# One sequence of scan rounds for all images, with a fixed share of other work between the sums of two rounds

## The chip, the core and the metric

The kernel runs on one core of a Trainium2 chip. The time is that of one launch on the device in microseconds, from several executions. All data are float32.

## What is computed

Eight images of 384 channels and 32 x 32 pixels go through four layers. Layer 0 is a Mamba block in both directions beside a local gate; its core, for each channel and each of 16 states, is a recurrence over the 1024 pixels:

```python
def step(h, inp):
    dA, dBu, c = inp
    h = dA * h + dBu
    return (h, jnp.einsum('bdn,bn->bd', h, c))
...
y = ys.transpose(1, 0, 2) + u * D_param
y = y * silu(z)
...
local_feat = jax.nn.sigmoid(conv + dw_b[None, :, None, None]) * x_norm
return x + res_scale * (global_feat + local_feat)
```

Layer 1 is a 1x1 convolution, a 3x3 depthwise one, another 1x1, a linear attention with eight heads and an MLP of 384 to 1536 to 384 with GELU. Layer 2 is a sum of depthwise convolutions (merged into one of 13 x 13), layer 3 a 1x1 and again a 13 x 13 depthwise convolution with GELU. Layers 2 and 3 come at the end for all images together.

## The kernel before

The program is written in a layer that records instructions with their data dependences, and then orders them on each engine by a list scheduler with its own model of times. Each engine (TensorE is PE, VectorE DVE, ScalarE ACT, GpSimd POOL, SyncE SP) then runs its list in order, and waits on semaphores where an input or a buffer isn't ready. Records made earlier have the higher priority, but what is ready first in the model goes first.

Four generators make the work of layers 0 and 1. A generator yields a number after each piece, its cost in units of about one dense product.

- `front(b)`, 90 units: the norm of image b, the input projection (`in`), the local gate (tiles `lc`, `lg`; conv3, L511; activation L615, products L618 and L619), the 1-D convolution (`ut`, `c1`, `uc`), the projections `xd` and `dt`, softplus (Abs, ReLU, Exp, Ln; L671 to L678) and the products for the scan (L683 to L689). It writes `dl_d`, `v_d`, `bc_d`, `ud_d`, `z_d` to device memory.
- `scan(b)`: the recurrence, in 12 units (two directions, two halves of 512 pixels, three groups of 128 channels) of four rounds each: 48 rounds an image. A round handles 4 of the 16 states for 128 channels, which gives 512 rows: two tiles (i = 0, 1) of two halves.
- `layer1(b)`, 325 units: out-projection (`op`), first 1x1 (`h`), depthwise (`dw`), second 1x1 (`c2`), keys and values (`kv`), queries (`q`), normalizer (`den`, `rz`, `rzb`), projection (`pj`), mean and variance (`mu`, `var`), and the MLP: 24 steps of a product `mf`, GELU (`hm`, L1062) and three products `mo` (L1064).
- `fold()` and `kernels` fold normalizations into weights and merge the convolutions' kernels, once.

A round of the scan, for each of the two tiles: ACT makes two exponentials `da` (L776), DVE a product `du` (L781, into PSUM) and two scans `hs` (L793), POOL multiplies by C in place (L802). Two rounds later PE adds over the states: four matmuls with a constant selector, each on 32 columns of the array (`sums`, L736), into one accumulator `acc`; in a unit's first round also an identity product (L741). After a unit's last round ACT (L746) or DVE (L749) takes `acc` away. There are four buffers of `da` (two rounds), eight of `hs` (four rounds), one of `du`, one of `acc`. Matmul results of the other work go to two PSUM buffers `mm` and three `mo`. The inputs of a depthwise or 1-D convolution are copied by DMA into `im` tiles, six of them, four for one convolution.

The driving loop runs the scan of image b and records, after each round, pieces of the front of image b+1 and of layer 1 of image b-1, in proportion to the rounds done. At the image's end it records all that is left, and the next image's scan starts anew, with its own loads. PE's order of sums against other products is left to the scheduler. The front of image 0 runs ahead of all, layer 1 of image 7 alone after all, then the convolutions (L316).

Of the kernel before, what the change touches and what calls it, by code (L numbers as in the profile page):

```python
# [36 lines left out]
N_A6, N_T2, N_S2, N_W, N_IM = 7, 11, 3, 4, 6  # L37
N_REP, N_DA, N_HS = 6, 4, 8
TP = H * (KP // 2)
PADW = KS // 2  # L40
# [334 lines left out]
def _layers01(tc, nc, B, xv, x2_d, dram, ident, mean_w, eps5, eps6, one, half, minus1, vec, bns, bnt,  # L375
# [12 lines left out]
    with ExitStack() as ctx:  # L388
# [30 lines left out]
        def const(ap, shape, tag):  # L419
            t = wp.tile(shape, FP, tag=tag, name=tag)  # L420
            nc.scalar.dma_start(t, ap)
            return t
# [10 lines left out]
        t1 = const(taps1, [P, 2 * NG, 32], "t1")  # L433
        selt = const(sel, [P, 32], "selt")
        neg_a = const(alog, [P, NG, NR], "neg_a")
        nc.scalar.activation(neg_a, neg_a, AF.Exp)
# [56 lines left out]
        def tick(everything=False):  # L493
            for e in list(late):
                e[0] -= 1
                if e[0] < 0 or everything:
                    late.remove(e)
                    e[1]()

        def dense(ps, w, m, rhs):  # L500
# [71 lines left out]
        def front(b):  # L572
# [36 lines left out]
            for h in range(2):  # L609
                for c in range(NC):  # L610
                    xr = t2(f"xr_{b}_{h}_{c}")
                    nc.sync.dma_start(xr, xv[b][:, c, bass.ts(h, HALF)])
                    ps = conv3(xn_d, b % 2, h, c, t3, f"lc_{b}_{h}_{c}")
                    lc = t2(f"lg_{b}_{c}_{h}")
                    nc.scalar.activation(lc, ps, AF.Sigmoid, bias=vec("dw_b0", c))  # L615

                    def local(h=h, c=c, lc=lc, xr=xr):
                        nc.vector.tensor_mul(rows(lc), rows(lc), xn[h][c])  # L618
                        nc.vector.scalar_tensor_tensor(xr, lc, rs, xr, ALU.mult, ALU.add)  # L619
                        nc.gpsimd.dma_start(x1v[b][:, c, bass.ts(h, HALF)], xr)  # L620

                    defer(1, local)
                    yield 3
# [70 lines left out]

        def scan(b):

            units = [
                (d, h, c)
                for d in range(2) for h in ((0, 1) if d == 0 else (1, 0)) for c in range(NC)
# [6 lines left out]
            def load_bc(k, r):  # L706
                d, h, _ = units[k]
                t = sp.tile([P, 2, HALF], FP, tag="bct", name=f"bct_{b}_{d}_{h}_{r}", bufs=4)
                for o in range(2):
                    src = bass.AP(  # L710
                        bc_d.tensor, bc_d[b, d, o * NST + 4 * r, h * HALF].offset,
                        [[0, 32], [L, 4], [1, HALF]],
                    )
                    nc.sync.dma_start(t[:, o, :], src)
                return t

            def load(k, i):

                d, h, c = units[k]
                ts = []  # L720
                for src_d, n in ((dl_d, "dlt"), (v_d, "vr")):
                    t = sp.tile([P, 2 * HALF], FP, tag="rep", name=f"{n}_{b}_{d}_{h}_{c}_{i}", bufs=N_REP)
                    for j in range(2):
                        src = bass.AP(
                            src_d.tensor, src_d[b, d, P * c + 32 * (2 * i + j), h * HALF].offset,
                            [[L, 32], [0, 4], [1, HALF]],
                        )
                        nc.sync.dma_start(t[:, bass.ts(j, HALF)], src)
                    ts.append(t)
                return ts  # L730

            def sums(k, r, hs, acc, y0, zt):
                d, h, c = units[k]
                cols = bass.ts(h, HALF)
                for j in range(4):
                    nc.tensor.matmul(  # L736
                        acc[32 * j : 32 * j + 32, :], selt, hs[j // 2][:, bass.ts(j % 2, HALF)],
                        start=(r == 0), stop=(r == NR - 1), skip_group_check=True,
                    )
                if r == 0:  # L740
                    nc.tensor.matmul(acc, ident, y0, start=False, stop=False, skip_group_check=True)  # L741
                if r < NR - 1:
# [11 lines left out]
            acc = y0 = zt = nxt = None  # L754
            for k, (d, h, c) in enumerate(units):
                cols = bass.ts(h, HALF)
                second = k % (2 * NC) >= NC
                for r in range(NR):
# [12 lines left out]
                    for i in range(2):  # L771
                        dlt, vt = now[i]
                        da = sp.tile([P, 2 * HALF], FP, tag="da", name=f"da_{b}_{k}_{r}_{i}", bufs=N_DA)
                        for j in range(2):
# [4 lines left out]
                            )  # L779
                        du = accp.tile([P, 2 * HALF], FP, tag="du", name=f"du_{b}_{k}_{r}_{i}")  # L780
                        nc.vector.tensor_mul(  # L781
# [5 lines left out]
                        if i == 0 and k and c == 0 and r == 0:  # L787
                            bct[NR - 1] = load_bc(k, NR - 1)
                        t = sp.tile([P, 2 * HALF], FP, tag="hs", name=f"hs_{b}_{k}_{r}_{i}", bufs=N_HS)
                        for j in range(2):  # L790
# [86 lines left out]
        def layer1(b):  # L877

            xx = []
            w = wtile(outproj_t, f"wo_{b}")  # L880
            for h in range(2):
                xh, gh = a6(f"xx_{b}_{h}"), a6(f"g_{b}_{h}")
                nc.sync.dma_start(xh, x1v[b][:, :, bass.ts(h, HALF)])
                nc.sync.dma_start(gh, gv[b][:, :, bass.ts(h, HALF)])
                xx.append(xh)
                for m in range(NC):
# [5 lines left out]
            w = wtile(c1_d, f"c1_{b}")  # L892
            for h in range(2):
                hh, mid = image6(f"hh_{b}_{h}")
# [195 lines left out]
        tick(everything=True)  # L1090
        rounds = 4 * NC * NR
        for b in range(B):
            work = []
            if b + 1 < B:
                work.append([front(b + 1), 90, 0])
            if b > 0:
                work.append([layer1(b - 1), 325, 0])
            if b == 0:
                work.append([fold(), 30, 0])
            if b == 1:  # L1100
                work.append([some(prepare, 7), 1, 0])
            elif b > 1:
                work.append([some(prepare, 6), 12, 0])
            need = sum(n for _, n, _ in work)
            done = 0
            for i, _ in enumerate(scan(b)):
                tick()

                while work and done < need * (i + 1) / (rounds - 1):
                    w = min(work, key=lambda w: w[2] / w[1])  # L1110
                    cost = next(w[0], None)
                    if cost is None:
                        work.remove(w)
                        continue
                    w[2] += cost
                    done += cost
            for w in work:
                for _ in w[0]:
                    tick()
            tick(everything=True)  # L1120
        for _ in prepare:
# [92 lines left out]
```

## Time and profile before

| | us |
|---|---|
| median of 3 runs (5799.74 to 5806.63) | 5803.92 |
| profiled execution: time | 5806.88 |
| profiled execution: span | 5805.1 |
| PE, DVE, ACT, POOL busy | 4813.5, 3677.1, 3064.5, 2892.9 |
| granted clock of TensorE, mean | 0.896 |

Times of a group are of single instructions; a float32 matmul appears as two entries (two passes). The ends of matmuls are modelled and overlap, so a group's busy time is shorter than count times mean. "Idle before" is what the engine waited ahead of the group, with what ended it.

### The profile page before, as it was taken

The page shows a single profiled execution, that of the slowest core. Times are in us where ns is not written, and L with a number is a line of the kernel's source. Part 1 is how long each engine was busy: PE and PEld are TensorE (multiplying, and loading weights), DVE is VectorE, ACT ScalarE, POOL GpSimd, SP SyncE. Part 2 cuts the span into 40 slices and gives each one's busy share as a digit, 9 for nine tenths or more (in the row PEclk, how much of TensorE's full clock was granted, in tenths as well). Part 3 has the DMA queues.
Part 4 walks back from the last instruction along what each step waited for, and adds up shares of the span by engine and source line. Part 5 has one row for each costly group of instructions (what it writes and reads, how often), then busy time and mean ns, then how long its engine had stood idle before and what let it go on. Part 6 is the DMA issues. An engine that isn't in the chain of part 4 may idle for free. (4 is left out here: it accounts for less than half of the span.)

```text
span 5805.1 us, 57844 instructions
## 1 busy us (share of the span) xinstructions
PE 4813.5 (83%) x19550; PEld 2091.8 (36%) x19550; DVE 3677.1 (63%) x3775; ACT 3064.5 (53%) x4116; POOL 2892.9 (50%) x1603
## 2 busy tenths in 40 slices
PE   4576579977988799879888997899779869899999
PEld 1121124322332243223322332233223324498498
DVE  0399997968687768776878786878678811011211
ACT  1656546874667557846784687468635613000211
POOL 3277676557554656565656564656466700110133
PEclk7687689988999899989999998899889989999999
DMA  9555476677567756764666467646643541366677
GB/s 299 185 176 178 145 247 194 230 188 216 187 197 202 216 173 193 168 204 134 191 205 189 141 175 186 190 140 176 179 145 120 135 96 45 95 165 158 196 166 150
DMA packets 528255, 1012.16 MB, mean 174 GB/s; under 512 B 60616, under 2 KB 196248, under 8 KB 527960
## 3 DMA queue, kind: packets, MB, share of 16 engines
q1 hardware_dynamic: 387952, 665.99, 38.5%
q0 software_dynamic: 71136, 248.53, 16.6%
q10 hardware_dynamic: 68872, 93.95, 5.1%
q8 instruction: 155, 2.54, 0.2%
q14 instruction: 140, 1.15, 0.1%
HBM read 763.86 MB, written 288.36 MB: 181 GB/s over the span
## 5 line engine op out<-in xcount | busy, mean ns | idle before, releaser
L802 POOL TENSOR_TENSOR hs<-hs,bct 128x1024 f32<-128x1024 f32 x768 | 2378.7, 3098 | 1180.4 <-DVE hs L793 665.8
L776 ACT ACTIVATE da<-dlt,neg_a 128x512 f32<-128x512 f32 x1536 | 1031.7, 714 | 848.8 <-DVE hs L793 756.8
L793 DVE TENSOR_TENSOR_SCAN hs<-da,carry,du 128x512 f32<-128x512 f32 x768 | 947.1, 1268 | 445.8 <-PE acc L736 211.0
L781 DVE TENSOR_TENSOR du<-vr,bct 128x1024 f32<-128x1024 f32 x768 | 1048.3, 1365 | 51.7 <-issue 21.7
L793 DVE TENSOR_TENSOR_SCAN hs<-da,du 128x512 f32<-128x512 f32 x768 | 901.2, 1208 | 153.9 <-ACT da L776 74.0
L736 PE MATMUL acc<-hs,selt 128*32 128x512 f32 x3072 | 736.5, 674 | 293.0 <-POOL hs L802 241.7
L1064 PE MATMUL mo<-hm,w 128*128 128x512 f32 x1152 | 562.5, 628 | 84.4 <-ACT hm L1062 60.8
L502 PE MATMUL mf<-ln,w 128*128 128x512 f32 x1152 | 545.7, 614 | 42.8 <-ACT dl L672 40.4
L736 PEld LDWEIGHTS acc<-hs,selt 128*32 128x32 f32 x3072 | 122.3, 115 | 722.2 <-POOL hs L802 391.6
L1064 PEld LDWEIGHTS mo<-hm,w 128*128 128x128 f32 x1152 | 214.9, 197 | 427.8 <-issue 255.1
L776 ACT ACT_TABLE_LOAD x265 | 340.0, 1283 | 39.2 <-DVE hs L793 26.7
L502 PEld LDWEIGHTS mf<-ln,w 128*128 128x128 f32 x1152 | 215.2, 194 | 358.9 <-issue 285.1
L316 PE MATMUL cv_b<-xt_b,toep 128*64 128x256 f32 x2688 | 304.5, 388 | 14.1 <-DVE xt_b L298 14.1
L316 PE MATMUL cv_a<-xt_a,toep 128*64 128x256 f32 x2688 | 304.6, 388 | 9.2 <-DVE xt_a L298 9.2
L502 PE MATMUL in<-xn,win 128*128 128x512 f32 x576 | 289.1, 633 | 26.0 <-ACT phi_k L874 24.2
L511 PE MATMUL dw<-dw_i,t3b 96*32 96x512 f32 x1152 | 238.0, 707 | 86.4 <-DMA dw_i<-h_d 86.3
L316 PEld LDWEIGHTS cv_b<-xt_b,toep 128*64 128x64 f32 x2688 | 282.5, 199 | 36.6 <-issue 16.2
L316 PEld LDWEIGHTS cv_a<-xt_a,toep 128*64 128x64 f32 x2688 | 282.4, 199 | 31.1 <-issue 10.4
L511 PE MATMUL lc<-lc_i,t 96*32 96x512 f32 x1152 | 218.1, 679 | 57.2 <-issue 28.8
L511 PE MATMUL c<-ut,t 128*32 128x512 f32 x768 | 195.2, 676 | 45.6 <-DMA ut<-u_d 32.1
L502 PE MATMUL op<-g,wo 128*128 128x512 f32 x288 | 143.1, 647 | 86.7 <-DMA g<-g_d 58.7
L1062 ACT ACTIVATE hm<-mf,biasf 128x512 f32<-128x512 f32 x192 | 130.7, 687 | 145.2 <-PE mf L502 143.5
(189 smaller groups left out, 5618.3 us busy)
## 6 DMA issues: line engine op xcount, KB each, us to landing
dlt<-dl_d SPq DMA_DIRECT2D x384, 256.0 KB, 4.5
vr<-v_d SPq DMA_DIRECT2D x384, 256.0 KB, 4.7
bct<-bc_d SPq DMA_DIRECT2D x256, 256.0 KB, 4.1
ut<-u_d SPq DMA_DIRECT2D x192, 257.5 KB, 5.0
lc_i<-xn_d SPq DMA_DIRECT2D x192, 228.8 KB, 4.9
dw_i<-h_d SPq DMA_DIRECT2D x192, 228.8 KB, 4.1
tp_d<-g_d POOLq DMA_DIRECT2D x64, 672.0 KB, 7.2
w<-w_d SPq DMA_DIRECT2D x64, 576.0 KB, 5.8
```

The costliest lines, as they stand in the source:

```text
L316: nc.tensor.matmul(ps[2 * H * e : 2 * H * (e + 1), 0:BW], tp[:, 2 * (g % (GB // 2)) + e, :, :, t].rearrange("p c j -> p (c j)"), rhs, star ...
L502: nc.tensor.matmul(ps, w[:, k, m * P : (m + 1) * P], rhs[k] if isinstance(rhs, list) else rhs[:, k, :], start=(k == 0), stop=(k == NC - 1),)
L511: nc.tensor.matmul(ps[32 * j : 32 * j + 32, :], lhs(j, i), rhs(j, i), start=(i == 0), stop=(i == taps - 1), skip_group_check=True,)
L736: nc.tensor.matmul(acc[32 * j : 32 * j + 32, :], selt, hs[j // 2][:, bass.ts(j % 2, HALF)], start=(r == 0), stop=(r == NR - 1), skip_group ...
L776: nc.scalar.activation(da[:, bass.ts(j, HALF)], dlt[:, bass.ts(j, HALF)], AF.Exp, scale=neg_a[:, g, r : r + 1],)
L781: nc.vector.tensor_mul(pairs(du), pairs(vt), bct[r][:, 0:1, :].to_broadcast([P, 2, HALF]),)
L793: nc.vector.tensor_tensor_scan(t[:, s][:, way], da[:, s][:, way], du[:, s][:, way], k_c if second else 0.0, ALU.mult, ALU.add,)
L802: nc.gpsimd.tensor_mul(pairs(t), pairs(t), bct[r][:, 1:2, :].to_broadcast([P, 2, HALF]))
L1062: nc.scalar.activation(hm, ps, AF.Gelu, bias=biasf[:, NC * i + f, :])
L1064: nc.tensor.matmul(acc[m], wb[:, f, m * P : (m + 1) * P], hm, start=(i == 0 and f == 0), stop=(i == FF // C - 1 and f == NC - 1),)
```

## The change

The program has one generator `scan()` that runs through the rounds of all eight images, with the buffers, the loads ahead and the two rounds of lag carried over the boundary. The driving loop takes one round at a time and then records each generator's share on its own, by the round's place between `lo` and `hi`: the front from round 0 to 43, layer 1 from 3 to 47. What it records is placed on PE behind the last sums recorded (`issue_after`), and the next sums behind the last PE instruction of each generator in that round (`order`); both are edges of order only, without a wait on a result. So on PE the sums of one round, one round's pieces, and the sums of the next round follow each other. `LAG` and `BEHIND` are constants that would loosen this.

Two further edits: the local gate's sigmoid is made from tanh, sigmoid(v) = (tanh(v/2) + 1)/2, with halved bias and residual scale (four small DVE products at the start); and layer 1 handles half 1 ahead of half 0 in its first two products, since the second direction's scan finishes half 1 first.

```diff
-                    nc.scalar.activation(lc, ps, AF.Sigmoid, bias=vec("dw_b0", c))
+                    nc.scalar.activation(lc, ps, AF.Tanh, bias=dwh[:, c, :], scale=0.5)
...
-                        nc.vector.tensor_mul(rows(lc), rows(lc), xn[h][c])
-                        nc.vector.scalar_tensor_tensor(xr, lc, rs, xr, ALU.mult, ALU.add)
+                        nc.vector.scalar_tensor_tensor(
+                            rows(lc), rows(lc), one, xn[h][c], ALU.add, ALU.mult
+                        )
+                        nc.vector.scalar_tensor_tensor(xr, lc, rsh, xr, ALU.mult, ALU.add)
...
-        def scan(b):
+        def scan():
             units = [
-                (d, h, c)
+                (b, d, h, c) for b in range(B)
                 for d in range(2) for h in ((0, 1) if d == 0 else (1, 0)) for c in range(NC)
             ]
...
+                after = between[-BEHIND] if len(between) >= BEHIND else []
                 for j in range(4):
-                    nc.tensor.matmul(
+                    ins = nc.tensor.matmul(
                         acc[32 * j : 32 * j + 32, :], selt, hs[j // 2][:, bass.ts(j % 2, HALF)],
                         start=(r == 0), stop=(r == NR - 1), skip_group_check=True,
                     )
+                    for o in after:
+                        order(ins.ins, o)
...
+                summed.append(ins.ins)
...
-            for h in range(2):
+            for h in (1, 0):
...
+        last = rounds - NR + 1
...
+                work.append([front(b + 1), 90, 0, last - 2, 0])
...
+                work.append([layer1(b - 1), 325, 3, rounds - 1, 0])
...
-            for i, _ in enumerate(scan(b)):
+            for i in range(rounds):
+                next(scans)
                 tick()
-                while work and done < need * (i + 1) / (rounds - 1):
-                    w = min(work, key=lambda w: w[2] / w[1])
...
-            for w in work:
-                for _ in w[0]:
-                    tick()
-            tick(everything=True)
+                ends = []
+                with tc.issue_after(summed[-1 - LAG]) if len(summed) > LAG else nullcontext():
+                    for w in list(work):
+                        gen, need, lo, hi, done = w
+                        at = len(traced())
+                        while done < need * (i + 1 - lo) / (hi - lo) or i >= hi:
+                            cost = next(gen, None)
...
+                        mine = [t for t in traced()[at:] if t.engine == mybir.EngineType.PE]
+                        if mine:
+                            ends.append(mine[-1])
+                between.append(ends)
```

## The prediction

> **What bounds the kernel now.** I read the stages first: the windows of the trace cut where a new image's scan starts (the first POOL product of each image gives the times), then the groups of the page, then the timeline of single rounds, then the waits of the tiles `hs`, `hm` and `dw_i`.
>
> ```profile
> core 0: us, PE busy (x) PEld busy (x) DVE busy (x) ACT busy (x) POOL busy (x), PEclk, DMA share, GB/s
> 0.00:227.10 227.10, 120.44 (x390) 34.41 (x392) 29.77 (x80) 67.10 (x90) 56.63 (x111) 0.73 0.87 275
> 227.10:738.20 511.10, 312.44 (x1000) 82.98 (x996) 442.17 (x424) 312.15 (x423) 330.10 (x157) 0.69 0.49 163
> ...
> 2461.10:3029.70 568.60, 481.74 (x1720) 174.49 (x1720) 440.89 (x435) 379.55 (x497) 330.92 (x157) 0.94 0.59 179
> ...
> 4170.10:4650.60 480.50, 393.71 (x1292) 146.18 (x1292) 392.73 (x386) 255.03 (x350) 311.25 (x121) 0.91 0.48 136
> 4650.60:5040.00 389.40, 314.11 (x912) 135.72 (x910) 32.17 (x52) 72.37 (x107) 22.88 (x30) 0.89 0.30 74
> 5040.00:5805.10 765.10, 734.39 (x5664) 620.14 (x5664) 129.07 (x192) 100.75 (x192) 153.67 (x182) 0.98 0.67 165
> ```
>
> Rows: front of image 0; scan of image 0; scan of image 4 (images 1 to 6 are like it: 581, 546, 596, 569, 566, 575 us); scan of image 7; layer 1 of image 7 alone; the convolutions. In the middle images PE is busy 85%, DVE 78%, ACT 67%: three engines close together, so 48 rounds of 11.8 us each are neither PE's nor DVE's sum alone. The spacing of the POOL products shows rounds from 7.6 us (nothing but DVE) to 42 us (image 4, 17th round: over 90 other matmuls stand between two sums). So work is lumped.
>
> ```profile
> L776 ACT ACTIVATE da<-dlt,neg_a 128x512 f32<-128x512 f32 x1536 | 1031.7, 714 | 848.8 <-DVE hs L793 756.8
> ...
> L793 DVE TENSOR_TENSOR_SCAN hs<-da,carry,du 128x512 f32<-128x512 f32 x768 | 947.1, 1268 | 445.8 <-PE acc L736 211.0
> ...
> L736 PE MATMUL acc<-hs,selt 128*32 128x512 f32 x3072 | 736.5, 674 | 293.0 <-POOL hs L802 241.7
> ...
> L776 ACT ACT_TABLE_LOAD x265 | 340.0, 1283 | 39.2 <-DVE hs L793 26.7
> ...
> L1062 ACT ACTIVATE hm<-mf,biasf 128x512 f32<-128x512 f32 x192 | 130.7, 687 | 145.2 <-PE mf L502 143.5
> ```
>
> Here a ring is seen: ACT's exponentials wait for DVE's scans (four `da` buffers, two rounds), DVE's scans wait for PE's sums (eight `hs` buffers, four rounds). One round in the timeline gives its prices:
>
> ```profile
> 2705.22 1.06 PE L736 MATMUL acc<-hs,selt 128*32 128x512 f32 x8
> ...
> 2706.22 7.99 PE L502 MATMUL q<-xx,wq 128*128 128x512 f32 x18
> ...
> 2706.49 2.45 DVE L793 TENSOR_TENSOR_SCAN hs<-da,carry,du 128x512 f32<-128x512 f32 x2 [3.62 <-PE acc L736]
> ...
> 2708.97 1.23 DVE L781 TENSOR_TENSOR du<-vr,bct 128x1024 f32<-128x1024 f32 x1
> ...
> 2710.34 2.45 DVE L793 TENSOR_TENSOR_SCAN hs<-da,carry,du 128x512 f32<-128x512 f32 x2
> ...
> 2714.14 1.07 PE L736 MATMUL acc<-hs,selt 128*32 128x512 f32 x8
> ```
>
> A round's sums take 1.06 us, with the change of tile on both sides about 1.56. DVE starts the first half's scan 0.2 us after them and ends the second half's 6.3 to 6.5 us after them. Eighteen entries in 7.99 us are nine matmuls: a dense group of three costs 2.57 us at full clock.
>
> ```profile
>   ACT hm L1062: 199.7, 123
> ...
>   DMA dw_i<-h_d: 208.7, 117
> ...
> DMA to landing us min/median/max: 3.0/4.1/7.9
> ```
>
> The first is what PE and its weight loads wait for GELU, the others are the depthwise loads of layer 1 and their time to landing.
>
> **The Trainium skill.** "TensorE: Matmul & The Clock Gate", section "Architectural detail", says ACT and DVE are strict FIFO and only PE's weight loads move ahead; the trace agrees (nothing above starts out of its engine's order), and my argument rests on it. Its "Part 1: The HAM clock gate" says an idle window of about 3.4 us halves PE's clock: in the tail, after the waits around `rzb`, weight loads come every 0.85 us and from 4857 us on every 0.43. "ScalarE: Activation LUTs", "What ACT_TABLE_LOAD costs", gives 1283 ns for a load, as here, and a drain beside it that I see no row for. Its "Table sets" puts tanh beside exp, which is what the sigmoid edit uses.
>
> **The change, part by part.**
>
> Sigmoid to tanh, with half scales (L615 to L619). The built orders count table loads: 776 before, 650 after. 126 x 1.283 = 162 us less on ACT, 20 us an image; these lie mostly in gaps where PE doesn't wait for ACT, so I take nothing (bounds 0 and 20 us an image). Product and sum become two scalar_tensor_tensor: L619 shows 0.82 us beside a median of 0.88 for L618, nothing. Four tiny DVE constants: nothing.
>
> One sequence of scans. Gone is each image's start: 8.4 us without a POOL product at most boundaries, and a first round of 14 to 31 us. The next image's `dlt`, `vr`, `bct` are now loaded during the old image's last rounds. About 25 us an image, and layer 1 begins three rounds late with half 1 first, so the wait for `g` (58.7 us in all images) goes.
>
> PE's order. I compared the instruction order of both programs. Before, other work between two sums is anywhere from 0 to 92 matmuls and sums are broken up by it; GELU products `mo` stand several groups after their `mf`. After, each gap holds one share (mostly 6 to 21 matmuls; the same list for images 1 to 6): in 20 gaps an image `mf`, then its `mo`, then the next sums. No instruction is added; waits are. What is queued behind `mo` is everything on PE, the sums too, and behind those DVE's scan four rounds on. And in the new order ACT's evictions of gap s mostly stand behind exponentials of round s+6 (median 6 for GELU; before 3), the furthest that the buffers allow: round s+6 waits for scan s+4, which waits for sums s. So in each gap PE waits for a chain that starts with its own last sums. With us after the end of sums s:
>
> - Plain GELU gap: scan 0.2 + 2.45, two exponentials 1.43, table load 1.28, GELU 0.69, PE start 0.1, `mo` 2.57, sums 1.56: 10.3. Four gaps, two of them with one exponential fewer: 39.8.
> - With the 1-D convolution: its matmuls to 2.1, two SiLU 1.38, load 1.28, exponentials 1.43, load 1.28, GELU to sums 4.92: 12.4. Four gaps; two more have exponentials of the second half between: 14.9. Sum 79.4.
> - With `dt`: 1.3, Abs and ReLU 4 x 0.68, load, two Exp 1.26, load, two Ln 1.43, load, then 4.92: 15.5. Three of 15.6, one 14.5, one with two sets 22: 83.3.
> - Two GELUs, an exponential and two loads between them: 17.2, 17.2, 14.2, 11.9: 60.5.
>
> That is 263 us in 19 gaps. The gap with both variances and the first GELU I put at 19. The other 28: two norm gaps and one `in` 20.7; out-projection and `h` 36 (PE's sum); depthwise three gaps 67 (h's eviction behind exponentials to 8.4, store 5.8, load 4.1, product 2.7, sums; then five convolutions at the 8.3 us that image 4 shows, 2555 to 2605 us, since six `im` buffers hold one and a half of them); `c2` 21; seven `kv` gaps 81 (phi and the copy stand behind round s+6: 8.2 to 14.6); `q`, `den` 41; `rzb`, `pj`, `mu` 42, DVE's extra 31 us falls there; an empty one 1.6. Sum 310. Image: 263 + 19 + 310 = 592, against a mean of 574 in the six before.
>
> A second way: layer 1 alone takes 389 us with its own stalls, in an order that still weaves `mf` ahead of `mo`; 48 sums at 1.56 and 12 identity matmuls at 0.86 add 85, the front 88 (PE's 482 of image 4 less the 394 of image 7): 562, with no exponential in GELU's way. I take 590, near the first.
>
> Whole: front 227.1. Image 0 has no layer 1 and is DVE's (442 busy of 511): 450, as its start and its waits shrink. Image 1 as the others plus the seven kernel preparations, 15 to 20 us of DVE (455 busy against 440): 610. Images 2 to 6: 5 x 590 = 2950. Image 7 without a front: its GELU gaps fall to 10 or 14 us: 515 (bounds 389 + 85 = 474, and 530). Rest unchanged, 389.4 + 765.1 = 1154.5. Sum 5906.6, against a span of 5805.1. The profiled run was 5806.9, the median 5803.9: the change of +101 on it gives 5905.
>
> **Rivals.**
>
> Faster: even gaps win. PE is then the bound, 482 us busy in image 4, and DVE's 441 lies under it. If the front's matmuls fill layer 1's own stalls (389 - 314 = 75 us) and the chains overlap, PE is busy nine tenths: an image takes 545 (bound 482), image 7 475, image 0 440, image 1 570: 227.1 + 440 + 570 + 2725 + 475 + 1154.5 = 5591. For it: rounds of 7.6 beside rounds of 42. Against: the order on ACT. It decides from an image time below 570.
>
> Slower by more: the idle parts of the gaps, 3 to 8 us, drop PE to half clock, so `mf` and `mo` cost up to 2.6 us more in a dozen gaps: 30 us an image, 5905 + 6 x 30 = 6085.
>
> No change: the boundary gain and the chains cancel, images at 570: about 5805.
>
> The order doesn't do what it says: excluded, both orders were listed.
>
> **Numbers.** The two slower cases 0.45 and 0.16, no change 0.05, faster 0.34. Less than 0.2% (12 us) is what a measurement of this kernel can't tell. Faster 0.34, same 0.05, slower 0.61. Range 5570 to 6090: it cuts the lower end of the faster case and the upper one of the half-clock case; the likeliest case alone is 5830 to 6010.
>
> **What would show it.** Right: MLP rounds (last 20 of an image) of 12 to 14 us, most PE idle ended by ACT `hm`, exponentials' idle by DVE, DVE's by PE sums; the depthwise rounds near 20; no gap between images. Wrong: MLP rounds of 9 to 10 us, PE busy above 90% in the middle images, or DVE idle under 50 us an image.

## The result and the profile after

The changed kernel took 6392.44 us (median of 4 runs, 6387.67 to 6405.85) beside 5805.16 us of the kernel before (median of four runs; the table of before has three of them): a ratio of 1.102, 95% interval 1.100 to 1.104. It is slower by 587 us, where the prediction had 101. The profiled execution has a span of 6391.1 us and a mean granted clock of 0.857 (before: 0.896).

The windows of the trace of after, cut where an image's scan starts: front, image 0, image 4, image 7, layer 1 of image 7, convolutions. The columns are those shown in the prediction: stretch, length, busy time of PE, PEld, DVE, ACT, POOL, then the granted clock, the DMA share and GB/s.

```profile
0.00:223.20 223.20, 117.61 (x388) 33.41 (x388) 30.41 (x84) 64.66 (x88) 56.61 (x111) 0.73 0.87 274
223.20:732.50 509.30, 297.60 (x1033) 84.60 (x1032) 439.57 (x427) 286.11 (x408) 331.42 (x160) 0.68 0.52 170
2725.50:3379.60 654.10, 501.05 (x1721) 185.65 (x1720) 436.30 (x435) 355.77 (x480) 337.12 (x156) 0.86 0.51 154
4701.30:5234.20 532.90, 407.35 (x1296) 152.58 (x1295) 384.10 (x382) 243.36 (x336) 317.20 (x120) 0.87 0.44 120
5234.20:5623.00 388.80, 322.38 (x940) 137.58 (x938) 33.98 (x54) 73.01 (x108) 22.97 (x30) 0.89 0.30 71
5623.00:6391.10 768.10, 736.50 (x5664) 620.75 (x5664) 129.04 (x192) 100.65 (x192) 157.12 (x182) 0.98 0.66 165
```

The ends of the program are as before. All the loss lies in the scans: images 1 to 6 take 664.6, 662.4, 666.0, 654.1, 659.6 and 662.1 us, image 7 takes 532.9. In image 4 DVE is busy as long as before (436 us; 441 before) and PE 19 us longer, but the image takes 85 us more: the engines have hardly more to do, and wait more.

The groups of the page of after, with the idle time and what ended it:

```profile
L802 ACT ACTIVATE da<-dlt,neg_a 128x512 f32<-128x512 f32 x1536 | 1034.5, 714 | 1420.6 <-DVE hs L819 1357.2
L819 DVE TENSOR_TENSOR_SCAN hs<-da,carry,du 128x512 f32<-128x512 f32 x768 | 943.8, 1267 | 727.3 <-PE acc L759 669.2
...
L1090 PE MATMUL mo<-hm,w 128*128 128x512 f32 x1152 | 676.5, 735 | 366.3 <-ACT hm L1088 366.3
L759 PE MATMUL acc<-hs,selt 128*32 128x512 f32 x3072 | 561.9, 676 | 176.1 <-POOL hs L828 161.9
```

The MLP's products in the kernel before:

```profile
L1064 PE MATMUL mo<-hm,w 128*128 128x512 f32 x1152 | 562.5, 628 | 84.4 <-ACT hm L1062 60.8
```

This is the ring closed. The exponentials waited 757 us for scans before, and now 1357; the scans with a carry waited 211 us for the sums, and now 669; the MLP's products waited 61 us for GELU, and now 366. How one turn goes is seen in the timeline of after, image 4, a gap with two GELUs:

```profile
3161.37 0.72 ACT L802 ACTIVATE da<-dlt,neg_a 128x512 f32<-128x512 f32 x1 [1.99 <-DVE hs L819]
...
3162.11 1.28 ACT L1088 ACT_TABLE_LOAD   x1
3163.41 0.69 ACT L1088 ACTIVATE hm<-mf,biasf 128x512 f32<-128x512 f32 x1
3164.11 1.28 ACT L802 ACT_TABLE_LOAD   x1
3164.15 2.84 PE L1090 MATMUL mo<-hm,w 128*128 128x512 f32 x6 [1.07 <-ACT hm L1088]
3165.41 0.72 ACT L802 ACTIVATE da<-dlt,neg_a 128x512 f32<-128x512 f32 x1
3166.15 1.28 ACT L1088 ACT_TABLE_LOAD   x1
3167.44 0.69 ACT L1088 ACTIVATE hm<-mf,biasf 128x512 f32<-128x512 f32 x1
3168.18 2.84 PE L1090 MATMUL mo<-hm,w 128*128 128x512 f32 x6 [1.19 <-ACT hm L1088]
3170.95 1.06 PE L759 MATMUL acc<-hs,selt 128*32 128x512 f32 x8
...
3172.22 2.33 DVE L819 TENSOR_TENSOR_SCAN hs<-da,du 128x512 f32<-128x512 f32 x2 [9.54 <-PE acc L759]
```

Read it upwards. DVE stood 9.5 us for the sums of 3170.95; these stood behind `mo`, `mo` waited for GELU, and each GELU stood behind an exponential and a table load, the first exponential behind a scan.

For a finer cut, the windows of image 4 at the ends of sums, one row for the gaps of one kind: `op` and `h`; `dw`; `c2`; `kv`; `q`, `lc`, `den`; `rzb`, `pj`, `mu`; variance with the first GELU; the 19 other MLP gaps.

```profile
2755.00:2798.50 43.50, 38.23 (x111) 14.90 (x107) 38.68 (x45) 16.31 (x26) 30.67 (x15) 0.96 0.62 201
2798.50:2880.90 82.40, 47.09 (x197) 13.45 (x193) 34.18 (x39) 19.22 (x32) 30.83 (x10) 0.73 0.61 182
2880.90:2902.20 21.30, 21.30 (x62) 8.53 (x61) 18.80 (x16) 12.19 (x17) 13.08 (x4) 1.00 0.43 138
2902.20:2984.60 82.40, 70.65 (x260) 33.88 (x259) 54.44 (x45) 47.87 (x71) 46.54 (x22) 0.93 0.25 84
2984.60:3038.00 53.40, 43.80 (x168) 14.08 (x168) 38.49 (x32) 24.00 (x38) 26.30 (x10) 0.85 0.68 210
3038.00:3083.40 45.40, 43.55 (x147) 15.68 (x150) 39.93 (x47) 14.73 (x22) 21.89 (x11) 0.85 0.52 157
3083.40:3115.10 31.70, 17.75 (x112) 8.71 (x108) 20.98 (x26) 17.43 (x24) 12.01 (x5) 0.68 0.31 104
3115.10:3388.10 273.00, 205.42 (x586) 70.05 (x582) 174.30 (x169) 191.76 (x234) 144.53 (x76) 0.87 0.48 159
```

Where PE fills the gap (`c2`, 21.3 of 21.3 us; `rzb` to `mu`, 43.6 of 45.4) the strict order costs little. It costs in the depthwise gaps (PE 47 of 82), at the variances (18 of 32) and in the MLP (205 of 273). In the table below the same cut is a mean over images 1 to 6, made from the times of all sums in the trace.

### The profile page after: what moved, and what is told of

It is laid out like the page before. It is cut to its first block, busy times and chain, and to the rows that moved or that the text cites. A ratio compares the mean times of both kernels' runs of the same rounds, so it can differ in the third digit from the quotient of the medians.

```text
span 6391.1 us, 57792 instructions
## 1 busy us (share of the span) xinstructions
PE 4863.3 (76%) x19550; PEld 2139.1 (33%) x19550; DVE 3637.5 (57%) x3779; ACT 2889.2 (45%) x3990; POOL 2958.0 (46%) x1603
## 5 line engine op out<-in xcount | busy, mean ns | idle before, releaser
L828 POOL TENSOR_TENSOR hs<-hs,bct 128x1024 f32<-128x1024 f32 x768 | 2440.0, 3177 | 1841.7 <-DVE hs L819 780.3
L807 DVE TENSOR_TENSOR du<-vr,bct 128x1024 f32<-128x1024 f32 x768 | 982.9, 1280 | 18.6 <-DMA vr<-v_d 6.2
L1090 PE MATMUL mo<-hm,w 128*128 128x512 f32 x1152 | 676.5, 735 | 366.3 <-ACT hm L1088 366.3
L759 PE MATMUL acc<-hs,selt 128*32 128x512 f32 x3072 | 561.9, 676 | 176.1 <-POOL hs L828 161.9
L519 PE MATMUL mf<-ln,w 128*128 128x512 f32 x1152 | 576.5, 644 | 81.6 <-ACT dl L691 59.7
L1090 PEld LDWEIGHTS mo<-hm,w 128*128 128x128 f32 x1152 | 248.1, 229 | 769.3 <-ACT hm L1088 517.4
L528 PE MATMUL dw<-dw_i,t3b 96*32 96x512 f32 x1152 | 265.5, 837 | 261.0 <-DMA dw_i<-h_d 140.6
L318 PEld LDWEIGHTS cv_b<-xt_b,toep 128*64 128x64 f32 x2688 | 282.7, 199 | 37.2 <-issue 16.5
L759 PEld LDWEIGHTS acc<-hs,selt 128*32 128x32 f32 x3072 | 89.4, 116 | 525.5 <-POOL hs L828 278.2
L1088 ACT ACTIVATE hm<-mf,biasf 128x512 f32<-128x512 f32 x192 | 131.9, 687 | 186.8 <-PE mf L519 184.5
L528 PEld LDWEIGHTS dw<-dw_i,t3b 96*32 96x32 f32 x1152 | 68.1, 139 | 440.1 <-issue 226.0
```

What stands on the lines that cost most here:

```text
L318: nc.tensor.matmul(ps[2 * H * e : 2 * H * (e + 1), 0:BW], tp[:, 2 * (g % (GB // 2)) + e, :, :, t].rearrange("p c j -> p (c j)"), rhs, star ...
L519: nc.tensor.matmul(ps, w[:, k, m * P : (m + 1) * P], rhs[k] if isinstance(rhs, list) else rhs[:, k, :], start=(k == 0), stop=(k == NC - 1),)
L528: nc.tensor.matmul(ps[32 * j : 32 * j + 32, :], lhs(j, i), rhs(j, i), start=(i == 0), stop=(i == taps - 1), skip_group_check=True,)
L759: ins = nc.tensor.matmul(acc[32 * j : 32 * j + 32, :], selt, hs[j // 2][:, bass.ts(j % 2, HALF)], start=(r == 0), stop=(r == NR - 1), skip ...
L807: nc.vector.tensor_mul(pairs(du), pairs(vt), bct[r][:, 0:1, :].to_broadcast([P, 2, HALF]),)
L828: nc.gpsimd.tensor_mul(pairs(t), pairs(t), bct[r][:, 1:2, :].to_broadcast([P, 2, HALF]))
```

## Experiments

Sixteen kernels were run. Ratios are to the kernel before on the same chip. The runs e1 to e4, e5 to e8, e9 to e12 and e13 to e16 stand on one chip each, so that a small difference between two of these groups compares two ratios. Unless a text says otherwise, a kernel is the changed one with the edit shown.

| run | time, us | ratio | 95% interval |
|---|---|---|---|
| after | 6392.44 | 1.1017 | 1.0998 to 1.1036 |
| e1_free | 5919.24 | 1.0288 | 1.0272 to 1.0304 |
| e2_share_behind | 5918.77 | 1.0286 | 1.0271 to 1.0301 |
| e3_sums_behind | 6050.82 | 1.0525 | 1.0497 to 1.0553 |
| e4_behind2 | 5955.17 | 1.0345 | 1.0330 to 1.0361 |
| e5_mo_later | 6053.19 | 1.0410 | 1.0384 to 1.0436 |
| e6_before_tanh | 5857.68 | 1.0077 | 1.0058 to 1.0097 |
| e7_exp_behind | 6132.32 | 1.0551 | 1.0531 to 1.0570 |
| e8_free_early_front | 5838.21 | 1.0037 | 1.0019 to 1.0054 |
| e9_dw_spread | 6041.59 | 1.0399 | 1.0380 to 1.0418 |
| e10_strict_all | 5790.29 | 0.9970 | 0.9959 to 0.9982 |
| e11_free_mo_later | 5867.51 | 1.0096 | 1.0079 to 1.0113 |
| e12_free_sigmoid | 5907.93 | 1.0164 | 1.0139 to 1.0190 |
| e13_strict_sigmoid | 6440.35 | 1.1087 | 1.1070 to 1.1104 |
| e14_mlp_packed | 6416.06 | 1.1037 | 1.1013 to 1.1061 |
| e15_free_dw_spread | 5892.36 | 1.0139 | 1.0122 to 1.0156 |
| e16_strict_late_front | 5637.36 | 0.9699 | 0.9684 to 0.9713 |

The strict kernels, us of an image by kind of gap (mean of images 1 to 6, from the ends of the sums; "edges" are the norm gaps, `in` and the last three):

| run | edges | op, h | dw | c2 | kv | q to den | rzb to mu | var | MLP | sum |
|---|---|---|---|---|---|---|---|---|---|---|
| predicted | 22.3 | 36 | 67 | 21 | 81 | 41 | 42 | 19 | 263 | 592 |
| after | 22.1 | 46.1 | 80.5 | 21.3 | 81.4 | 50.6 | 44.7 | 31.3 | 282.8 | 660.9 |
| e14 | 46.7 | 42.2 | 84.0 | 21.3 | 81.1 | 50.2 | 45.0 | 31.5 | 266.3 | 668.4 |
| e7 | 23.4 | 48.4 | 75.8 | 21.3 | 81.3 | 51.9 | 49.5 | 29.5 | 245.5 | 626.6 |
| e5 | 37.6 | 48.3 | 82.2 | 21.3 | 81.3 | 49.7 | 45.3 | 27.6 | 217.5 | 610.7 |
| e9 | 22.2 | 49.7 | 65.3 | 20.4 | 94.5 | 34.7 | 37.1 | 34.8 | 245.5 | 604.2 |
| e10 | 25.8 | 56.3 | 97.6 | 25.5 | 103.5 | 37.4 | 42.2 | 23.0 | 154.6 | 565.9 |
| e16 | 36.1 | 53.2 | 66.6 | 20.4 | 92.6 | 31.1 | 38.8 | 29.2 | 179.4 | 547.5 |

### Is it the order? (e1 to e4)

e1 takes both kinds of order edges away: PE's list is left to the scheduler, the single sequence and the shares stay.

```diff
-                    for o in after:
-                        order(ins.ins, o)
...
-                with tc.issue_after(summed[-1 - LAG]) if len(summed) > LAG else nullcontext():
+                with nullcontext():
```

> The changed kernel with both kinds of order edges taken out: one sequence of rounds, the same shares, tanh, half 1 first, and PE's order left to the scheduler. Theory A (the strict order makes PE wait for chains that begin with its own last sums): 5650 to 5830 us, a little under the kernel before, as the image starts are gone. Theory B (the one sequence with its loads and late layer 1 is itself what costs): over 6200 us. Part of each: between.

e2 keeps only the second edge (a share behind the sums), e3 only the first (the sums behind the last share), e4 sets `BEHIND = 2`, so that the sums may pass one share.

> Only the edges that hold a round's share behind the last sums are kept; the sums need not wait for the share. Theory A: the harm comes from sums held behind a share, so this is like the free one, 5650 to 5850 us. Theory B: over 6200 us.

> Only the edges that hold the sums behind the share of the round are kept. Theory A: the harm is all here, 6300 to 6450 us, and GELU still stands a median of 6 rounds of exponentials ahead in ACT's order. Rival A2 (it takes both edges, since without the other one PE can bring later shares ahead): under 6100 us.

> Sums held behind the share of one round earlier (BEHIND = 2), so that the sums can fill the wait between mf and mo. Theory A: most of the loss is got back, 5850 to 6050 us. Theory B: over 6200 us.

The order edges carry most of the loss: 7.3 points of 10.2 are gone without them (e1). The share's edge alone does nothing (e2 is e1 within its interval), the sums' edge alone adds 2.4 points, and both together 7.3, as the rival A2 of e3 had it. One share of slack in front of the sums gives 6.7 of the 7.3 back (e4, inside its expectation). So most of the loss needs TensorE held on both sides. But 2.9% stayed without any edge: e1 and e2 are above the 5830 and 5850 us that their first theories allowed. The windows of e1 in image 4 show where, two groups of four rounds late in the image:

```profile
2908.70:2981.80 73.10, 63.12 (x167) 21.24 (x166) 44.26 (x45) 59.95 (x74) 36.47 (x28) 0.95 0.61 192
2981.80:3059.80 78.00, 69.07 (x180) 22.93 (x178) 39.76 (x41) 64.42 (x79) 33.77 (x23) 0.93 0.42 140
```

A round takes 18 to 20 us there, with ACT busy 0.82 and DVE 0.5 to 0.6; there are 20 and 23 table loads in these rounds. They hold both the next image's softplus and the MLP's GELU, since each share is now spread over its own range of rounds.

### Softplus beside GELU (e8, and e11, e12, e15 on its base)

e8 is e1 with the front spread over rounds 0 to 26 in place of 0 to 43.

```diff
-                work.append([front(b + 1), 90, 0, last - 2, 0])
+                work.append([front(b + 1), 90, 0, 26, 0])
```

> One sequence without order edges (as in the free run, ratio 1.029), with the front spread over rounds 0 to 26 in place of 0 to 43, so that softplus of the next image does not fall on GELU's rounds. Theory D (ACT is the bound in the free run's rounds 36 to 43, by table loads for Exp, Ln and GELU in turn): ratio 0.97 to 1.00. Rival (the late layer 1, half 1 first or the loads over the boundary cost it): stays at 1.02 to 1.03.

2.5 of the 2.9 points go. The ratio came near the expectation and just missed it: the single sequence with even shares, without order, is no gain even so. The edit moves the whole front, so it doesn't single out softplus: PE's wait for the front's loads of `ut`, the input of its 1-D convolution, falls with it, from 124.0 us in e1 to 15.0 in e8 (32.1 before). How the 2.5 points divide between the two is not shown. Three further edits on this base did not beat the kernel before either: e11 with the MLP's products one piece later (the edit of e5 below), e12 with the sigmoid in place of the tanh, e15 with the depthwise pieces spread (the edit of e9).

> No order edges (as in e8, front in rounds 0 to 26), and the MLP's products recorded one piece behind their GELU. Theory A (without the edges the products no longer bar the sums for long, since the scheduler may put the sums ahead): little left to win, ratio 0.985 to 1.003. Rival R (program order still places the products straight behind their dense in TensorE's queue, and the MLP rounds lose 1 to 1.5 us each to it, 19 x 7 of them = 130 to 200 us): ratio 0.965 to 0.98, faster than both kernels.

> e8 with the sigmoid put back in the local conv in place of the tanh and its two larger VectorE operations. Theory A (the tanh's 0.8%, measured alone on the kernel before, adds to the rest): ratio 0.993 to 0.999, that is, one sequence with early front is worth a little by itself. Rival R (the tanh's loss came from where its pieces fell in the planner's order of the kernel before, and not from the operation): ratio 1.001 to 1.006, as e8.

> No order edges and the front in rounds 0 to 26 (as in e8), with the depthwise pieces spread as in e9. Theory A (the wait for the padded map is a cost of the strict order; with the sums free to pass, there is little to win): ratio 0.995 to 1.005. Rival R (the pieces behind the map also hold up TensorE's queue in program order without the edges): ratio 0.97 to 0.99, faster than both kernels.

All three are slower than e8, by 0.6, 1.3 and 1.0%, and all missed both theories' numbers. Why e11 and e15 lose is not known; e12 is taken up below.

### What the strict order waits for (e5, e7)

e5 keeps the order and records the three `mo` of a piece after the `mf` of the next one, so GELU has a whole gap's time.

```diff
                         dense(ps, wa, f, xns[h])
+                        if held:
+                            products(False)
...
-                        for m in range(NC):
-                            nc.tensor.matmul(
...
+                        held.append((i, f, wb, hm))
```

> The changed kernel, both order edges kept, with the three products mo of a GELU recorded in the next MLP piece ahead of its mf, so that a round's sums stand between mf and its mo and GELU has a whole round. Theory A1 (PE's wait for GELU inside a gap is the largest part of the loss): MLP gaps fall from a mean of 14.4 us to about 10, ratio to the kernel before 1.04 to 1.06. Rival A3 (the exponentials and table loads on ACT make the gaps, wherever mo stands): ratio 1.085 or more.

e7 leaves TensorE's list alone and changes ScalarE's: the exponentials of round n are ordered behind ScalarE's last instruction of each share of round n-3, so that a GELU has no more than about four rounds of exponentials ahead of it, and not six.

```diff
-                            nc.scalar.activation(
+                            ins = nc.scalar.activation(
...
+                            n = 4 * k + r - AHEAD
+                            for o in shares[n] if n >= 0 else []:
+                                order(ins.ins, o)
```

> The changed kernel, both PE order edges kept, and on ACT the exponentials of a round held behind ACT's last instruction of the share three rounds earlier, so that GELU of a gap stands behind exponentials that need no scan after this gap's sums (4 rounds ahead, not 6). Theory A2 (the ring through the exponentials makes the chains long): ratio 1.04 to 1.06. If mf, GELU and mo in one gap are what costs: 1.085 to 1.10.

Both came as their theory said. The windows of the 19 MLP gaps of image 4, first e5, then e7 (after: 273.00 us, clock 0.87):

```profile
2959.10:3160.10 201.00, 184.69 (x582) 65.11 (x574) 157.48 (x149) 178.45 (x217) 121.81 (x69) 0.95 0.59 189
```

```profile
3025.40:3256.90 231.50, 195.41 (x589) 66.98 (x582) 171.13 (x166) 174.26 (x221) 140.10 (x74) 0.90 0.57 187
```

It is one loss seen from two sides: GELU comes late since exponentials stand ahead of it, and its lateness counts since the sums stand behind `mo`. Mending the first alone (e7) gives 42 us of the 273 back, mending the second alone (e5) 72; of these some 15 return at the image's end, where e5's last products now stand ("edges" in the table). In e5 PE is also busy 21 us less for nearly the same matmuls (582 entries, 586 in after), at a granted clock of 0.95 and not 0.87.

### The depthwise gaps (e9) and the packing of the MLP (e14)

The timeline of after at the first depthwise gap of image 4:

```profile
2797.46 1.07 PE L759 MATMUL acc<-hs,selt 128*32 128x512 f32 x8
...
2798.71 2.33 DVE L819 TENSOR_TENSOR_SCAN hs<-da,du 128x512 f32<-128x512 f32 x2
...
2813.93 2.33 DVE L819 TENSOR_TENSOR_SCAN hs<-da,du 128x512 f32<-128x512 f32 x2
...
2816.29 0.72 ACT L802 ACTIVATE da<-dlt,neg_a 128x512 f32<-128x512 f32 x1 [1.90 <-DVE hs L819]
2816.92 0.67 ACT L924 ACTIVATE hh<-h,bias 128x512 f32<-128x512 f32 x1
...
2817.66 0.38 ACTq L547 DMA_DIRECT2D h_d<-hh  x1
2823.97 12.01 SPq L558 DMA_DIRECT2D dw_i<-h_d  x9
2828.06 6.18 PE L528 MATMUL dw<-dw_i,t3b 96*32 96x512 f32 x23 [21.61 <-issue]
...
2834.97 1.22 DVE L819 TENSOR_TENSOR_SCAN hs<-da,du 128x512 f32<-128x512 f32 x1 [17.37 <-PE acc L759]
```

From the end of the sums (2798.5) the last eviction of `h` ends at +19.1 us, its store is issued, the load back follows at +25.4, and the conv starts at +29.5. The eviction is late since ScalarE's list weaves it between exponentials, each waiting for a scan, and DVE had five pairs of scans still to do (the first and the fifth are shown). e9 starts the depthwise pieces 18 units later behind the store and gives each conv 8 units in place of 3.

```diff
+            yield 18
...
-                    yield 3
+                    yield 8
...
-                work.append([layer1(b - 1), 325, 3, rounds - 1, 0])
+                work.append([layer1(b - 1), 373, 3, rounds - 1, 0])
```

> The changed kernel in its strict order, with one thing moved: image b-1's depthwise pieces start later behind the transfer of the padded map (a pause of 18 units after it is stored and loaded again, and 8 instead of 3 between two conv pieces), so that a conv's weights and inputs have landed a round before the conv stands in TensorE's order. Theory A (a gap's excess is what its own last wait adds, and gaps add up): the four gaps that hold these convs go from 82 us of an image to about 60, the rest of the image stays, and the time falls by 6 images x 15 to 22 us = 90 to 130 us, to 6260 to 6300, ratio 1.08 to 1.09. Rival R (the wait only moves: the same evictions and transfers are then late in the next gap): within 30 us of the changed kernel, ratio 1.095 to 1.105.

It went much further: 350 us, not 90 to 130. The windows of e9, image 4: the depthwise gaps with two empty ones, and the MLP, now in 16 gaps behind the variances:

```profile
2642.20:2708.40 66.20, 52.03 (x250) 15.77 (x250) 59.30 (x57) 33.72 (x50) 51.54 (x17) 0.92 0.82 239
...
2930.50:3165.40 234.90, 185.75 (x515) 65.44 (x516) 151.94 (x144) 169.19 (x208) 123.40 (x67) 0.90 0.51 161
```

The table splits the 57 us of an image: 15 in the depthwise gaps, as expected; 37 in the MLP; 16 in `q` to `den` less 13 in `kv`, where the front's convolutions now stand beside `kv` pieces. e14 was to tell whether the MLP's part is its number of gaps. It gives a GELU piece 5 units in place of 6, so that the 24 pieces stand in 17 gaps as in e9, and leaves three gaps empty after them.

> The changed kernel with the MLP's pieces at 5 units each in place of 6, so that image b-1's 24 GELU pieces stand in 17 gaps and not 20, and three gaps at the end of an image are empty; all else where it was. Theory A (a gap costs by the exchange between TensorE and ScalarE that it holds, whatever its work; two GELUs in one gap cost less than in two): the 19 MLP gaps of 273 us go to 16 of about 235 and three empty ones of 4 to 9 us, so 15 to 25 us an image less, 90 to 150 us in all, ratio 1.075 to 1.087. Rival R (the sum of the MLP's work counts, not its gaps; e9's gain came from the depthwise pieces and what follows them): within 40 us, ratio 1.095 to 1.105.

The time did not fall. The MLP column, which counts the three empty gaps, fell by 16.5 us, but the last gaps of the image and the first of the next grew by 24.6. Part of it is seen in ACT's timeline of e14 at the end of image 2: an exponential that had run ahead waits for the next image's first input load.

```profile
2083.16 1.33 ACT L802 ACTIVATE da<-dlt,neg_a 128x512 f32<-128x512 f32 x2 [24.32 <-DMA dlt<-dl_d]
```

This load took 29.8 us to land, beside the stores of layer 1's output `x_d` (more of these stores below). In image 4, beside which these stores are fast, e14 takes 645.6 us from start to start and after 654.1; of the other five images four are 6 to 33 us longer in e14 and one is 8 us shorter.

So fewer gaps with GELUs are worth some 16 us of e9's 37, as long as nothing else comes due earlier. What gave the other 20 us of e9's MLP is not settled. One part is seen: three of the front's six pieces of the 1-D convolution that share gaps with GELUs in after and in e14 stand ahead of the MLP's gaps in e9. In image 4, the first three MLP gaps of e14, which hold these pieces, take 44.0 us; the last three of e9, with as many GELUs and no such piece, take 34.4.

### Together (e10, e16)

e10 has the edits of e5, e7, e8's early front and e9 in the strict order; e16 is the same with the front over rounds 0 to 43, as in the changed kernel.

> The strict order kept, with four of its late sources moved at once: the exponentials held behind ScalarE's share three rounds before (as in e7), the MLP's products one piece behind their GELU (as in e5), the depthwise pieces spread (as in e9), and the next image's front in rounds 0 to 26 (as in e8). Theory A (the loss is a sum of separate late arrivals in the order): e5 took 6.1% off and e7 4.7%; with e9's 1.5 to 2% and e8's 2.5% the sum is about 15% of before's time less the overlap of e5 and e7 (both shorten the same MLP gaps): ratio 0.97 to 1.02. Rival R (a fixed alternation costs by itself, since every round ends with an exchange between TensorE, ScalarE and VectorE in both directions): above 1.03 however the sources are placed.

> e10 with the front spread over rounds 0 to 43 again. Theory A (as in the free order, the early front is worth 1.4%: softplus and GELU apart): ratio 1.005 to 1.015. Rival R (in the strict order the front's pieces only move the exchanges into the gaps of the attention, which became long in e10, 23 to 27 us): ratio 0.97 to 0.99, faster than both kernels.

e10 is on a level with the kernel before, and e16 is faster than both kernels: 5637 us, 3.0% below before. The early front, right in the free order, is wrong in the strict one: the table shows e10's `dw` and `kv` gaps 31 and 11 us longer than e16's, for 25 us won in the MLP. The windows of e16, image 4, MLP:

```profile
2740.80:2919.40 178.60, 172.88 (x508) 62.19 (x508) 130.03 (x126) 162.35 (x200) 106.98 (x62) 0.96 0.58 186
```

PE is busy 97% of it. The page of e16 shows the ring open:

```profile
L803 ACT ACTIVATE da<-dlt,neg_a 128x512 f32<-128x512 f32 x1536 | 1008.4, 713 | 440.2 <-DVE hs L823 276.4
L823 DVE TENSOR_TENSOR_SCAN hs<-da,carry,du 128x512 f32<-128x512 f32 x768 | 946.2, 1268 | 315.4 <-PE acc L760 138.9
...
L1091 PE MATMUL mo<-hm,w 128*128 128x512 f32 x1152 | 574.0, 636 | 46.4 <-ACT hm L1105 44.3
...
L1105 ACT ACTIVATE hm<-mf,biasf 128x512 f32<-128x512 f32 x192 | 132.0, 688 | 221.5 <-PE mf L520 220.1
```

`mo` waits 44 us for GELU and not 366, and GELU waits 220 us for PE (184.5 in after). The strict order is thus not a loss in itself. It makes every wait inside a share a wait of the scan, and once the shares hold few, it is faster than every kernel without it that was run. But no run has all of e16's edits without the order edges, so what the edges themselves add to them is not shown.

### The tanh (e6, e13)

e6 is the kernel before with the tanh edit alone, e13 the changed kernel with the sigmoid put back.

> The kernel before with the tanh edit alone. Prediction's step: nothing, ratio 0.995 to 1.000 (43 table loads fewer, 55 us of ACT, mostly hidden). Rival: the edit lets the scheduler reorder and costs or gains more than 1%.

> The changed kernel with the sigmoid put back in the local conv (the sums and their order unchanged). Theory A (the tanh saves table loads, as in the free order, where putting the sigmoid back cost 1.3%): slower than the changed kernel by 0.5 to 1.5%, ratio 1.105 to 1.118. Rival R (the two larger VectorE operations of the tanh cost more than the loads, as on the kernel before): faster than the changed kernel by 0.5 to 1%, ratio 1.09 to 1.096.

The table loads in the traces: 776 before and 687 in e6; 730 in e13 and 650 after; 716 in e12 and 628 in e8. So it saves 80 to 90 loads of 1.283 us everywhere, as the Trainium skill's "ScalarE: Activation LUTs", "Table sets" has it (tanh beside exp). The time follows in two of the three: 0.6% in the strict order (the ratios 1.1087 and 1.1017; the loads saved are 103 us, 1.8%), 1.3% in the free one (e8 and e12). On the kernel before it is 0.8% slower, where 0.995 to 1.000 was expected. There the scheduler's model decides the whole order, and a small edit may reshuffle it; that this is the reason is not shown.

## Why the prediction was wrong

The direction and the ring were right; the size was not. In the prediction's own sum the excess of 485 us over 5906.6 is: front -4, image 0 +59, image 1 +55, images 2 to 6 +354, image 7 +18, the rest +2.

- **The step that failed** is the sum of an image, "263 + 19 + 310 = 592". It measured 661. Right within 3 us were the edges, `c2`, `kv` and `rzb` to `mu`. Mis-sized were `op` and `h` (36, measured 46.1), `dw` (67, 80.5), `q` to `den` (41, 50.6), the variances (19, 31.3) and the MLP (263, 282.8). These 65 us are nearly all of the 69. Where nothing else came in, the priced chain holds: the four gaps with two GELUs took 59.6 us in image 4, at a clock of 1.00, against 60.5.
- **What the sizes lacked.** The chain of the depthwise gap was priced with "h's eviction behind exponentials to 8.4"; it took 19.1, since DVE was not caught up at the sums but had two and a half rounds of scans to do. That gap took 37.0 us in image 4. In `op` the wait for `g`, which was to go, is still 54.1 us in all (58.7 before). In `q` to `den` the local conv's load of its taps was left out, for which PE sat idle 9.6 us in image 4. For the variances 19 us was set without a chain; the timeline has table loads and exponentials between square root and its neighbours, and PE waits 7.5 us for the first, 3.4 for the second. Of the MLP's 20 us some 10 are a load that no chain had: in images 1, 2, 3, 5 and 6 PE waits 11 to 14 us in one gap for `ut`. Image 4, shown above, has no such wait, and its MLP took 273.0. The larger errors all have the same sign: a chain is priced by the steps one has thought of. The lines of after (the first is of image 3, the last two are for half clock, below):

```profile
2604.24 4.48 PE L528 MATMUL c<-ut,t 128*32 128x512 f32 x12 [13.03 <-DMA ut<-u_d]
...
3007.77 5.35 PE L528 MATMUL lc<-lc_i,t 96*32 96x512 f32 x24 [9.60 <-DMA t<-in_taps]
...
3097.25 2.07 PE L581 MATMUL var_b<-var_r,spread 128*128 128x128 f32 x8 [7.49 <-ACT var_r L578]
...
3104.13 2.08 PE L581 MATMUL var_b<-var_r,spread 128*128 128x128 f32 x8 [3.37 <-ACT var_r L578]
...
3325.22 2.84 PE L1090 MATMUL mo<-hm,w 128*128 128x512 f32 x6 [2.35 <-ACT hm L1088]
...
3382.59 4.48 PE L1090 MATMUL mo<-hm,w 128*128 128x512 f32 x6 [2.33 <-ACT hm L1088]
```

- **Why the load of `ut` is late.** The three stores of layer 1's output `x_d` at the end of each half of the MLP take up to 28 us to land in after, and what is issued beside them is slow too (`ut` 24 to 26 us). In all eighteen traces (before, after, e1 to e16) the last of the three takes 16 to 29 us for six of the eight images, and no store takes more than 10 us for the other two, images 3 and 7; the scan of image 4 runs beside layer 1 of image 3. The kernel writes image b at column 6 + 38 b of rows of 312 numbers of four bytes, so within a row only images 3 and 7 begin at a multiple of 32 bytes. No run moved these columns, so that this is the reason is not shown. The wait for `ut` stays in e5 and e7 (123.8 and 101.1 us) and is all but gone in e9 and e16 (7.7 and 6.7).
- **Half clock was no rival, but a part.** "The idle parts of the gaps ... drop PE to half clock" was priced at 30 us an image on top. Of the 1152 `mo` entries 292 last over 900 ns in after, 54 before, 126 in e5 and 75 in e16, beside a median of 592 ns in all four; PE's busy time on `mo` grew from 562.5 to 676.5 us, 16 us for each of the seven images whose MLP stands in a scan. The last two lines above are of two gaps with one `mf`, one GELU and its `mo`, after the same wait of 2.3 us: the first takes 9.8 us at a granted clock of 1.00, the second 11.4 at 0.85. The Trainium skill's "TensorE: Matmul & The Clock Gate", "Part 1: The HAM clock gate", puts half clock after an idle window of about 3.4 us; here the length of one wait doesn't tell it, and no run varied the clock by itself. With its 30 us an image the prediction's sum is 6085, still 300 us under what was measured, so the clock is the smaller part of the miss.
- **"About 25 us an image" for one sequence** was wrong. Without the order, images 1 to 6 take 593 us from start to start in e1 and 569 in e8 (means), where they took 572 before (the prediction's 574 is 572 by its own list). But in e8 image 0 takes 566 us, with more of DVE's work in it (485 us; 442 before), where it took 511 before. So nothing of the 25 us is found in either, and where it went is not shown. In the sum of the strict image the 25 us was not used as a term, so it is not the source of the 485.
- **Image 0 at 450**: DVE's 440 us of work took 509 us, as before's 511. Its start and waits did not shrink; no run separates them. e16 leaves it as it was.
- **Tanh at nothing**: it is worth 0.6% in the strict order, some 5 us an image, inside the bounds of 0 and 20.
- **The faster rival** needed chains that overlap. The change doesn't have them; e16 does, with images of 547 us (the rival said 545) and image 7 at 454.

What would show it right was mostly there: PE's waits for GELU, exponentials' idle by DVE, DVE's by PE sums, no gap at the boundary. The MLP gaps came out a little longer (14.9 us on average over images 1 to 6, 14.4 in image 4, against 12 to 14), and of the depthwise gaps, put near 20, one took 37.0 and one 25.6 us in image 4.

## What to carry to other kernels

An order by hand makes every wait inside a share a wait of whatever follows: before fixing it, record consumers a share later than their producers, and put the queues of the other engines in the same order, or the edges close a ring. The same edit can help in one order and hurt in another (the early front: 2.5% won in the free order, 2.7% lost in the strict one), so pieces are to be tried in the order they will run in. The Trainium skill's "Perfetto Trace Analysis", "Optimization Strategy", says that interleaving regimes with different limits may help; here a fixed interleaving of the same work cost 10.2% or gained 3.0%, by what waits its shares held. When a stage is priced as a chain of waits, look for the steps left out: here nearly all of them added, and a lower clock came on top of them.

## What was not expected

Two order edges that cost 0 and 2.4 points alone cost 7.3 together (e2, e3 over e1). Spreading six convolutions over more gaps took 350 us off, and only 15 of its 57 us an image were in the gaps it was made for. TensorE's mean `mo` went from 628 to 735 ns with the same instructions, beside longer waits. And the store of layer 1's output is slow for the same six images in every kernel, which decided whose loads came late.
